# First attention: the row sums and the division of a unit go behind the next unit's weight scores

## The chip, the cores and the metric

The kernel runs on one core of a Trainium2 chip. It has a matrix engine (TensorE, PE in the profile; PEld are its weight loads), a vector engine (VectorE, DVE), an engine for activation functions (ScalarE, ACT), a general engine (GpSimd, POOL) and an engine that here issues transfers (SyncE, SP). Each engine runs its own instructions in the order in which the program gives them, and waits where an instruction needs another engine's result or a buffer that is still in use. The metric is the device time of one execution in microseconds (us).

## The reference, cut to what matters

The program is a decoder of two layers on an input of 8 batches of 256 tokens and 512 features. Each layer has a self-attention, a second mixing step and a feed-forward part, each added to the input and normalized. The change lies in the self-attention of the first layer, a differential attention with 32 score heads of 16 features and 4 value heads of 32:

```python
q = (x @ Wq.T).reshape(bsz, tgt, 2 * H, HD)
k = (x @ Wk.T).reshape(bsz, tgt, 2 * KVH, HD)
v = (x @ Wv.T).reshape(bsz, tgt, KVH, 2 * HD)
k = jnp.repeat(k, NREP, axis=2)
v = jnp.repeat(v, 2 * NREP, axis=2)
...
scores = jnp.einsum('bhqd,bhkd->bhqk', q, k) * scale
...
scores = jnp.where(causal, scores, jnp.finfo(scores.dtype).min)
probs = jax.nn.softmax(scores, axis=-1)
attn_out = jnp.einsum('bhqk,bhkd->bhqd', probs, v)
attn1 = attn_out[:, 0::2]
attn2 = attn_out[:, 1::2]
...
attn = attn1 - lambda_full * attn2
attn = attn * jax.lax.rsqrt(jnp.mean(attn * attn, axis=-1, keepdims=True) + EPS) * ln_w
attn = attn * (1.0 - LAMBDA_INIT)
...
return attn @ Wo.T
...
x = _layernorm(x + _L0_attn_ref(x, L0_attn_Wq, L0_attn_Wk, L0_attn_Wv, L0_attn_Wo, L0_attn_lambda_q1, L0_attn_lambda_k1, L0_attn_lambda_q2, L0_attn_lambda_k2, L0_attn_ln_w), axis=-1)
```

Two later self-attentions, of the second layer, use the same code path of the kernel with other inputs.

## The kernel before, in words

`causal_attention` (line 1238 on) is written once and called three times: as "a" for the first attention, "s" for the second layer's attention and "r" for its last part. The change concerns "a". There the work is cut into 64 units. A unit is one batch of 256 tokens and four score heads, which sit on the four quarters of the 128 partitions; eight units make a batch (`upb` is 8), sixteen a group of two batches.

A unit passes through three stages at three times, each in another turn of the loop over `u`:

- `maxima(u)`: the scores with queries on the partitions (ps_q, line 1300), copied out by ACT (`rows`, line 1309), masked by POOL (line 1311) and reduced to the largest value of each query by DVE (`neg`, line 1320). At the end of a batch `split` turns these maxima into three bf16 terms (lines 1327 to 1334, six small DVE steps), and `turn` brings them to the other layout with TensorE (ps_n, line 1342).
- `weights(u - 9)`: the scores again, with keys on the partitions (ps_k, line 1363), less the maxima (line 1372); ACT takes the exponential (`pT`, line 1380), POOL masks it (line 1381) and adds two of its blocks (line 1391), so that one product can sum the rest.
- `products(u - 10)`: the weights times the values (ps_pv, line 1406), then the weights times ones (line 1416), which gives the sum of each row; DVE takes the reciprocal (line 1424) and divides. In "a" this is `gather`: an even unit's result is written with line 451; an odd unit's, times minus lambda, goes to `second` (line 454), and POOL adds it (line 455). After a batch's last unit `finish` prepares the row norm: ACT squares (line 575), TensorE sums (line 527), POOL takes the roots (line 556, 8 columns each, four steps on different turns), ACT widens them (line 552), TensorE turns them and DVE multiplies (line 572); then the batch's two output blocks (ps_o) are made, added to x and normalized (`add_norm_later`).

ps_q and ps_k have the same name of buffer, "sc", of four banks, and there is one. So each waits until ACT has emptied the other. The buffer of ps_pv, one bank, is also single, except in the last batch.

The loop writes the order by hand, by Python at the time of the build. In each turn of `u` it gives: events of "start", `maxima`, some filling work, `products` (through `sums`), events of "mid", `weights`, more filling work (projections of the next batches, output blocks, transposes; a cost is kept for each and a budget `rate` of at least 2.4 a turn), `turn` after a batch's end, the rest of the filling, the reduction of the maxima, `split`, and events of "end". `at(n, place, f)` books `f` for n turns later. After 64 turns there are no more maxima, and ten more turns finish the last batch in another order: weights, products, "mid", filling.

In the last group the context is transposed too (`turn_context`): the eight even tiles go to a buffer that stays, the eight odd ones to `cT`, and each is written to memory by a transfer that SP issues (line 442).

Of the kernel before, what the change touches and what calls it, by code (L numbers as in the profile page):

```python
# [17 lines left out]
F32 = mybir.dt.float32  # L18
BF16 = mybir.dt.bfloat16
AF = mybir.ActivationFunctionType  # L20
ALU = mybir.AluOpType
# [3 lines left out]
P = 128  # L25
B, S, D = 8, 256, 512
NT = B * S // P
# [3 lines left out]
KB = D // P  # L31
# [22 lines left out]
def decoder_kernel(ctx: ExitStack, tc: tile.TileContext, a: dict, out: bass.AP):  # L54
    nc = tc.nc
# [236 lines left out]
    def diff_attention(xh, ch):  # L292
# [142 lines left out]
        def turn_context(work, pools, i):  # L435
            t = order[i]
            if t % 2:
                c = work.tile([P, KB, P], F32, tag="cT", name="cT")
            else:
                c = ch[:, :, t // 2, :]  # L440
            turned(pools, c, cx.pop(i))
            nc.sync.dma_start(out=ctx_d[:, :, t * P : (t + 1) * P], in_=c)
            if i + 2 < NT:
                load_context(work, i + 2)

        def gather(work, pools, at, yT, n, c, o, r):

            k = c // 2 % 2 * 2 + c // 4
            y = yT[:, k, :]
            if c % 2 == 0:  # L450
                nc.vector.tensor_tensor(y, o, r, ALU.mult)
                return
            d = work.tile([P, S], F32, tag="second", name="second")
            nc.vector.scalar_tensor_tensor(d, o, nlam, r, ALU.mult, ALU.mult)
            nc.gpsimd.tensor_tensor(y, y, d, ALU.add)
            if n < B - 1:
                return
            sq = squares(n)[:, k, :]

            def sums():  # L460
                ps = pools.tile([P, 2, 4], F32, tag="mm", name="ps_ss")
                for i in range(2):
                    nc.tensor.matmul(
                        ps[:, i, :], lhsT=sq[:, i * P : (i + 1) * P], rhs=quad, start=True, stop=True
                    )
                rr = small.tile([P, 2 * 4], F32, tag="rr", name="rr")
                nc.vector.tensor_scalar(
                    rr, ps.rearrange("p i t -> p (i t)"), 1.0 / 32, EPS, ALU.mult, ALU.add
                )
                wide = work.tile([P, 2 * 4, 32], F32, tag="wide2", name="wide2")  # L470
                at(0, "end", lambda: nc.gpsimd.tensor_tensor(rr, rr, neg_half[:, :8], ALU.pow))
                at(1, "mid", lambda: nc.scalar.copy(wide, rr.unsqueeze(2).broadcast_to([P, 8, 32])))
                at(1, "fill", [(TR / 2, lambda: scale(wide))])

            def scale(wide):
                pt = pools.tile([P, 2, P], F32, tag="mm", name="pt_rr")
                for i in range(2):
                    nc.tensor.transpose(
                        pt[:, i, :], wide[:, 4 * i : 4 * i + 4, :].rearrange("p t d -> p (t d)"), ident
                    )  # L480
                nc.vector.tensor_tensor(y, y, pt.rearrange("p i q -> p (i q)"), ALU.mult)

                if k == 1:
                    last.extend(out_tile(work, pools, 2 * n + i, yT, at) for i in range(2))
                    for steps in last:
                        at(0, "fill", steps[: KB - 1])
                elif k == KB - 1:
                    for steps in last:
                        at(0, "fill", steps[KB - 1 :])

            at(1, "mid", lambda: nc.scalar.activation(sq, y, AF.Square))
            at(1, "fill", [(0.4, sums)])

        last = []
# [11 lines left out]
        def finish(work, pools, t0, yT, at):  # L506
# [4 lines left out]


            apart = 1 if t0 == NT - 4 else 2
            wide = {}
            sq = squares(t0 // 2)

# [55 lines left out]
                nc.vector.tensor_tensor(y, y, pt, ALU.mult)  # L572
                at(1, "fill", out_tile(work, pools, t0 + i, yT, at))

            at(1, "start", lambda: nc.scalar.activation(sq, yT, AF.Square))
            at(1, "fill", [(0.7, sums)])
            return cost

        causal_attention("a", prepare, finish, 8, gather)
# [658 lines left out]
    def causal_attention(name, prepare, finish, upb=KB, gather=None):  # L1238
# [18 lines left out]
        with ExitStack() as st:  # L1257
# [6 lines left out]
            start = ExitStack()  # L1264
# [128 lines left out]
            def products(u):  # L1393

                g, b, c = unit(u)
                v = groups[g][2]
                p = pT.pop(u)

                late = u >= units - upb
                spare = late and u % 2  # L1400
                ps = (pools if spare else ps_pv).tile(
                    [P, 2, S], F32, tag="mm" if spare else "pv", name="ps_pv"
                )
                for j in range(2):
                    for s in range(4):
                        nc.tensor.matmul(  # L1406
                            ps[32 * s : 32 * s + 32, 0, j * P :],
                            lhsT=v(2 * b + j, 4 * c + s),
                            rhs=p[:, 1, s, :] if j else p[:, 0:3:2, s, :],
                            start=(j == 0),  # L1410
                            stop=(j == 1),
                        )
                first = p[:, 0:3:2] if late else p[:, 0:4:3]
                for j in range(2 if late else 1):
                    for s in range(4):
                        nc.tensor.matmul(  # L1416
                            ps[32 * s : 32 * s + 32, 1, j * P :],
                            lhsT=ones_v,
                            rhs=p[:, 1, s, :] if j else first[:, :, s, :],
                            start=(j == 0),  # L1420
                            stop=(j == 1 or not late),
                        )
                r = work.tile([P, S], F32, tag="rsum", name="rsum")
                nc.vector.reciprocal(r, ps[:, 1, :])  # L1424
                if c == 0:
                    yT[u // upb] = work.tile([P, KB, S], F32, tag="yT", name="yT_b")
                if gather:
                    gather(work, pools, at, yT[u // upb], u // upb, c, ps[:, 0, :], r)
                else:
                    nc.vector.tensor_tensor(yT[u // upb][:, c, :], ps[:, 0, :], r, ALU.mult)  # L1430

            upg = 2 * upb
            units = upg * NG
# [9 lines left out]
            def at(slots, place, f):  # L1443


                if place == "due mid":
                    at(slots, "mid", lambda: insort(queue, f, key=lambda piece: piece[0]))
                elif place == "fill":
                    after.append((now[0] + slots, f))
                    after.sort(key=lambda piece: piece[0])  # L1450
                else:
                    events.setdefault((now[0] + slots, place), []).append(f)

            def happen(place):
                for f in events.pop((now[0], place), []):
                    f()
# [43 lines left out]
                return most  # L1500

            def sums(u):
                nonlocal per_batch
                if lag <= u < units + lag:
                    products(u - lag)
                    if (u - lag) % upb == upb - 1:
                        n = (u - lag) // upb
                        per_batch = finish(work, pools, 2 * n, yT.pop(n), at)

            begin(0)  # L1510
            need(0)
# [5 lines left out]
            for u in range(units + lag + 2):  # L1517
                now[0] = u
                happen("start")

                rate = max(2.4, pressure(u) + per_batch / upb)
                if u < units:
                    largest = maxima(u)
                    short = max(0.0, min(0.8, rate - 1.8))
                    if rate > 2.7:
                        short += (rate - 2.7) / 2
                    left = fill(left + short)
                    sums(u)
                    happen("mid")
                    if u >= wait:  # L1530
                        weights(u - wait)
                    if u % upg == upb and u // upg + 1 < NG:
                        begin(u // upg + 1)
                    left = fill(left + rate - short - MM) - need(u + 1)

                    if u and u % upb == 0:
                        turn(u // upb - 1)
                    left = fill(left + MM)
                    largest()
                    if u % upb == upb - 1:  # L1540
                        split(u // upb)
                else:

                    if u < units + wait:
                        weights(u - wait)
                    sums(u)
                    happen("mid")
                    left = fill(left + rate) - need(u + 1)
                    if u == units:
                        turn(B - 1)  # L1550
                happen("end")
# [759 lines left out]
```

## Time and profile before

The runs took 2078.91, 2085.25 and 2088.3 us, a median of 2085.25. The profile is of an execution of its own:

| | |
|---|---|
| profiled execution | 2086.01 us |
| span from its first to its last instruction | 2084.3 us |
| PE / PEld busy | 1926.3 / 1123.2 us |
| DVE / ACT / POOL busy | 1231.7 / 617.3 / 853.7 us |
| mean granted TensorE clock | 0.982 |
| first attention, ps_q of unit 0 to the last division | 13.3 to 447 us |
| units 10 to 62, ps_q to ps_q | 54.02 to 388.71 us |

How to read it: a matmul's row has a start and a modelled end, and matmuls overlap, so the start-to-start time tells more than the duration. A number in square brackets in the order of time is the idle time of that engine before the instruction, and the name behind the arrow is the one whose result ended it. A line number is that of the kernel's listing; several operations share the line of a helper (208 is the helper that feeds projections by columns). POOL's durations are rough.

### The profile page before, as it was taken

What the parts mean: (1) busy time and instruction counts of PE and PEld (TensorE: products, weight loads), DVE (VectorE), ACT (ScalarE), POOL (GpSimd) and SP (SyncE); (2) the same over time, 40 slices, a digit from 0 to 9 for tenths busy, and PEclk for the clock granted to TensorE, in tenths of its full rate; (3) what the DMA queues carried; (4) which work ended last, traced back from release to release, by engine and by line L of the source; (5) the groups of instructions that cost most, each with busy time, mean ns of one, the idle gap of its engine ahead of it and who ended that gap; (6) DMA issues with size and microseconds to landing.
All of it is one profiled execution on the core that took longest, in us unless ns stands there. A gap on an engine that the chain in (4) does not pass through costs nothing. (4 is left out here: it accounts for less than half of the span.)

```text
span 2084.3 us, 46208 instructions
## 1 busy us (share of the span) xinstructions
PE 1926.3 (92%) x20068; PEld 1123.2 (54%) x20068; DVE 1231.7 (59%) x1876; ACT 617.3 (30%) x790; POOL 853.7 (41%) x945
## 2 busy tenths in 40 slices
PE   7979999889999999999969999998999999988885
PEld 5545555444443445656635545544878778454443
DVE  4677777658888975122225757457343442536887
ACT  4555555530000003211114334431101011245552
POOL 2677777647555833000014545344000000216763
PEclk9999999999999999999989999999999999999998
DMA  6899933316124126223122212002000000160000
GB/s 227 314 397 391 382 126 78 87 36 235 31 71 150 58 93 205 70 89 120 56 92 78 82 32 82 3 2 91 33 21 31 22 29 1 53 223 12 30 24 31
DMA packets 137467, 218.17 MB, mean 105 GB/s; under 512 B 27376, under 2 KB 52080, under 8 KB 137264
## 3 DMA queue, kind: packets, MB, share of 16 engines
q1 hardware_dynamic: 130800, 194.88, 27.0%
q0 software_dynamic: 6464, 20.32, 2.9%
q8 instruction: 160, 2.62, 0.5%
q14 instruction: 43, 0.35, 0.1%
HBM read 104.42 MB, written 123.34 MB: 109 GB/s over the span
## 5 line engine op out<-in xcount | busy, mean ns | idle before, releaser
L1424 DVE RECIPROCAL rsum<-ps_pv 128x256 f32<-128x256 f32 x128 | 224.4, 1753 | 223.3 <-PE ps_pv L1416 223.2
L178 PE MATMUL ps_y<-kv,wt 128*128 128x512 f32 x640 | 280.1, 596 | 5.2 <-POOL kv L620 2.7
L1380 ACT ACTIVATE pT<-ps_k 128x1536 f32<-128x1536 f32 x128 | 185.7, 1451 | 239.0 <-PE ps_k L1372 232.1
L1320 DVE TENSOR_REDUCE neg<-rows 128x12 f32<-128x1536 f32 x128 | 222.9, 1741 | 47.4 <-POOL rows L1311 47.4
L1309 ACT COPY rows<-ps_q 128x1536 f32<-128x1536 f32 x128 | 184.1, 1438 | 160.5 <-PE ps_q L1300 100.0
L1381 POOL TENSOR_SCALAR_AFFINE_SELECT pT<-pT 128x1024 f32<-128x1024 f32 x128 | 141.1, 1102 | 186.0 <-ACT pT L1380 185.9
L1311 POOL TENSOR_SCALAR_AFFINE_SELECT rows<-rows 128x1024 f32<-128x1024 f32 x128 | 141.0, 1101 | 159.8 <-ACT rows L1309 159.4
L178 PEld LDWEIGHTS ps_y<-kv,wt 128*128 128x128 f32 x640 | 120.8, 191 | 156.4 <-issue 137.0
L1391 POOL TENSOR_TENSOR pT<-pT 128x512 f32<-128x512 f32 x112 | 147.4, 1316 | 9.3
L1217 POOL DMA_INDIRECT first_h<-ys,slots x32 | 33.3, 1041 | 261.5 <-DMA ys<-y_m 253.9
L208 PE MATMUL ps_f<-xT,w_l1a 128*32 128x256 f32 x2048 | 124.0, 386 | 1.7 <-ACT xT L233 1.7
L1104 DVE TENSOR_TENSOR h_b<-h_b,pg 128x352 f32<-128x352 f32 x36 | 18.7, 520 | 147.2 <-ACT h_b L1103 146.4
L146 POOL TENSOR_SCALAR rstd<-bn_mv 128x1 f32<-128x1 f32 x80 | 16.6, 207 | 213.4 <-DVE bn_mv L152 209.8
L1416 PE MATMUL ps_pv<-pT,ones_v 128*32 128x256 f32 (+1 forms) x1152 | 86.2, 376 | 15.3 <-POOL pT L1391 15.1
L1125 PE MATMUL po_m<-dn,hT 128*128 (+1 forms) x216 | 98.8, 594 | 0.6 <-ACT hT L1115 0.5
L658 DVE TENSOR_REDUCE yc<-z 128x64 f32<-128x512 f32 x128 | 86.1, 673 | 5.7 <-POOL w_l1a L659 5.2
L208 PEld LDWEIGHTS ps_f<-xT,w_l1a 128*32 128x32 f32 x2048 | 62.7, 111 | 47.9 <-issue 9.6
L1300 PE MATMUL ps_q<-kz,qT 32*128 32x128 f32 x1536 | 61.5, 289 | 17.1 <-ACT pT L1380 13.8
L1300 PEld LDWEIGHTS ps_q<-kT,qT 32*128 32x128 f32 x1536 | 48.6, 186 | 51.1 <-ACT pT L1380 17.5
L1300 PE MATMUL ps_q<-kT,qT 32*128 32x128 f32 x1536 | 60.8, 287 | 14.1 <-ACT pT L1380 8.6
L1300 PEld LDWEIGHTS ps_q<-kz,qT 32*128 32x128 f32 x1536 | 49.2, 188 | 45.7 <-ACT pT L1380 32.1
L1363 PE MATMUL ps_k<-qT,kT 32*128 32x256 f32 (+1 forms) x1024 | 69.6, 358 | 4.5 <-ACT pT L1380 2.2
(386 smaller groups left out, 3620.4 us busy)
## 6 DMA issues: line engine op xcount, KB each, us to landing
xs<-zero SPq DMA_DIRECT2D x8, 4352.0 KB
ys<-zero SPq DMA_DIRECT2D x8, 4352.0 KB
filters<-in_L_xattn_k SPq DMA_DIRECT2D x4, 2560.0 KB
first_h<-xs SPq DMA_DIRECT2D x36, 256.0 KB
ys<-y_m SPq DMA_DIRECT2D x36, 256.0 KB
gu<-in_L_ffn_gate_up_proj SPq DMA_DIRECT2D x3, 2816.0 KB
wt<-filters SPq DMA_DIRECT2D x32, 256.0 KB
sorted_x<-zero SPq DMA_DIRECT2D x1, 5120.0 KB
```

Source lines behind the costliest of these rows:

```text
L178: nc.tensor.matmul(ps, lhsT=lhsT(k), rhs=rhs(k), start=(k == 0), stop=(k == n - 1))
L208: nc.tensor.matmul(ps[cs], lhsT=lhsT[:, cs], rhs=rhs, start=start, stop=stop)
L1125: nc.tensor.matmul(po, lhsT=hT[:m, i, :], rhs=dn[i][:m, bass.ds(e, 1), :], start=(i == 0), stop=(i == len(FCH) - 1),)
L1300: nc.tensor.matmul(block[:, s, j, :], lhsT=q(rows, c, b * S + i * P, P), rhs=k(rows, c, b * S + keys * P, P), start=True, stop=True,)
L1309: nc.scalar.copy(d.rearrange("p j s k -> p s j k"), block)
L1311: nc.gpsimd.affine_select(out=rows, in_=rows, compare_op=ALU.is_ge, fill=-FAR, base=0, pattern=[[0, 8], [-1, P]], channel_multiplier=1,)
L1320: return lambda: nc.vector.tensor_reduce(neg[u // upb % 2][:, :, :, c], d, AX.X, ALU.max, negate=True)
L1380: nc.scalar.activation(p[:, 0:3].rearrange("p j s q -> p s j q"), block, AF.Exp)
L1381: nc.gpsimd.affine_select(out=p[:, 0:2].rearrange("p j s q -> p (j s) q"), in_=p[:, 0:2].rearrange("p j s q -> p (j s) q"), compare_op=ALU ...
L1391: nc.gpsimd.tensor_tensor(p[:, 3], p[:, 1], p[:, 2], ALU.add)
L1416: nc.tensor.matmul(ps[32 * s : 32 * s + 32, 1, j * P :], lhsT=ones_v, rhs=p[:, 1, s, :] if j else first[:, :, s, :], start=(j == 0), stop= ...
L1424: nc.vector.reciprocal(r, ps[:, 1, :])
```

## The change

`products` is cut in two. The values products stay where they were. The ones products, the reciprocal, the new yT tile and the division (with `gather`) become a function `divided` that `products` returns; `sums` returns it together with the batch's `finish` as `rest`. In "a" the main loop calls `rest`, and then the events of "mid", after `weights`; in "s" and "r", and in the last ten turns of "a", it calls it at once, so the order there is the old one.

The row norm's start moves with it: for all batches of `finish` but the last it handles (`hurry`, batch 6), Square is booked for the end of the next turn instead of its start, and the sums product for the turn after that instead of the next. Three buffer counts change: yT has three in "a" instead of two, cT one instead of two, and the last batch's widened roots, "wide2", use the buffers of "wide".

```diff
-                c = work.tile([P, KB, P], F32, tag="cT", name="cT")
+                c = work.tile([P, KB, P], F32, tag="cT", name="cT", bufs=1)
...
-                wide = work.tile([P, 2 * 4, 32], F32, tag="wide2", name="wide2")
+                wide = work.tile([P, 2 * 4, 32], F32, tag="wide", name="wide2")
...
+            hurry = t0 == NT - 4
...
-            at(1, "start", lambda: nc.scalar.activation(sq, yT, AF.Square))
-            at(1, "fill", [(0.7, sums)])
+            at(1, "start" if hurry else "end", lambda: nc.scalar.activation(sq, yT, AF.Square))
+            at(1 if hurry else 2, "fill", [(0.7, sums)])
...
-                first = p[:, 0:3:2] if late else p[:, 0:4:3]
-                for j in range(2 if late else 1):
-                    for s in range(4):
-                        nc.tensor.matmul(
-                            ps[32 * s : 32 * s + 32, 1, j * P :],
-                            lhsT=ones_v,
-                            rhs=p[:, 1, s, :] if j else first[:, :, s, :],
-                            start=(j == 0),
-                            stop=(j == 1 or not late),
+                def divided():
+                    first = p[:, 0:3:2] if late else p[:, 0:4:3]
+                    for j in range(2 if late else 1):
+                        for s in range(4):
+                            nc.tensor.matmul(
+                                ps[32 * s : 32 * s + 32, 1, j * P :],
+                                lhsT=ones_v,
+                                rhs=p[:, 1, s, :] if j else first[:, :, s, :],
+                                start=(j == 0),
+                                stop=(j == 1 or not late),
+                            )
+                    r = work.tile([P, S], F32, tag="rsum", name="rsum")
+                    nc.vector.reciprocal(r, ps[:, 1, :])
+                    if c == 0:
+                        yT[u // upb] = work.tile(
+                            [P, KB, S], F32, tag="yT", name="yT_b", bufs=3 if name == "a" else 2
                         )
-                r = work.tile([P, S], F32, tag="rsum", name="rsum")
-                nc.vector.reciprocal(r, ps[:, 1, :])
-                if c == 0:
-                    yT[u // upb] = work.tile([P, KB, S], F32, tag="yT", name="yT_b")
-                if gather:
-                    gather(work, pools, at, yT[u // upb], u // upb, c, ps[:, 0, :], r)
-                else:
-                    nc.vector.tensor_tensor(yT[u // upb][:, c, :], ps[:, 0, :], r, ALU.mult)
+                    if gather:
+                        gather(work, pools, at, yT[u // upb], u // upb, c, ps[:, 0, :], r)
+                    else:
+                        nc.vector.tensor_tensor(yT[u // upb][:, c, :], ps[:, 0, :], r, ALU.mult)
+
+                return divided
...
-                if lag <= u < units + lag:
-                    products(u - lag)
+                if not lag <= u < units + lag:
+                    return lambda: None
+                divided = products(u - lag)
+
+                def rest():
+                    nonlocal per_batch
+                    divided()
                     if (u - lag) % upb == upb - 1:
                         n = (u - lag) // upb
                         per_batch = finish(work, pools, 2 * n, yT.pop(n), at)
+
+                return rest
...
-                    sums(u)
-                    happen("mid")
+                    rest = sums(u)
+                    if name != "a":
+                        rest()
+                        happen("mid")
                     if u >= wait:
                         weights(u - wait)
+                    if name == "a":
+                        rest()
+                        happen("mid")
...
-                    sums(u)
+                    sums(u)()
                     happen("mid")
```

More of the change, by code (lines that the diff above doesn't have):

```diff
@@ L1502, in sums @@
             def sums(u):
-                nonlocal per_batch
-                if lag <= u < units + lag:
-                    products(u - lag)
+                if not lag <= u < units + lag:
[4 more added lines that the diff above has]
+                    divided()
                     if (u - lag) % upb == upb - 1:
```

## The prediction, made before the run

> **What bounds the kernel now.** I read the share of busy time first (PE 92%, so time can only come out of TensorE's idle parts), then the 40 slices, where the first attention, up to about 447 us, holds the low digits the change can reach, then the waits by line there, then the order of time of single units. The change touches no loop outside this attention, so its window decides; this is that window, units 10 to 62, and what the rest of the kernel has beside it.
>
> ```profile
> 54.00:388.70 334.70, 300.58 (x5528) 170.27 (x5524) 247.88 (x265) 187.35 (x180) 247.10 (x230) 0.99 0.74 269
> 388.70:447.00 58.30, 50.34 (x798) 29.13 (x794) 40.70 (x56) 25.92 (x31) 33.13 (x34) 1.00 0.23 67
> ```
>
> The columns are the stretch, its length, and the busy time of PE, PE's weight loads, DVE, ACT and POOL. In 53 units of 6.31 us PE idles for 34 us; no engine is full. So a chain bounds a unit, and the order of time of unit 52 shows which (start, duration, engine, line, output and inputs, idle time before it and who ended it):
>
> ```profile
> 319.15 0.95 PE L1300 MATMUL ps_q<-kz,qT 32*128 32x128 f32 x24
> 320.17 1.44 ACT L1309 COPY rows<-ps_q 128x1536 f32<-128x1536 f32 x1 [0.96 <-PE ps_q L1300]
> ...
> 320.62 1.27 POOL L1391 TENSOR_TENSOR pT<-pT 128x512 f32<-128x512 f32 x1
> ...
> 321.94 0.64 PE L1416 MATMUL ps_pv<-pT,ones_v 128*32 128x256 f32 x8 [0.50 <-POOL pT L1391]
> 322.51 0.71 PE L1363 MATMUL ps_k<-qT,kz 32*128 32x256 f32 x8
> 322.65 1.76 DVE L1424 RECIPROCAL rsum<-ps_pv 128x256 f32<-128x256 f32 x1 [2.32 <-PE ps_pv L1416]
> ...
> 323.74 1.45 ACT L1380 ACTIVATE pT<-ps_k 128x1536 f32<-128x1536 f32 x1 [2.13 <-PE ps_k L1372]
> ...
> 325.84 0.76 PEld L1300 LDWEIGHTS ps_q<-kz,qT 32*128 32x128 f32 x24 [0.41 <-ACT qT L1567]
> ```
>
> The two score products share one buffer. The next ps_q waits for the exponential (L1380) to empty it, ps_k for the copy (L1309). The copy ends at 321.61, yet ps_k starts at 322.51: PE stands in order behind the ones products, and these wait for POOL's sum (L1391), which ends at 321.89. That is 0.90 us in which ACT waits for nothing but PE's order. The waits of the window say the same (total, times, longest):
>
> ```profile
> ACT pT L1380 <- PE ps_k L1372: 96.4, 52, 3.1
> DVE rsum L1424 <- PE ps_pv L1416: 75.6, 43, 3.7
> ...
> PEld ps_q L1300 <- ACT pT L1380: 31.3, 35, 2.1
> ...
> PEld ps_pv L1416 <- POOL pT L1391: 17.8, 28, 0.9
> ```
>
> At unit 49 nothing stood in the way: ps_q at 301.19, ps_k at 303.70, next ps_q at 306.43. So a unit has two halves with floors: A, ps_q to ps_k, 2.51 us (1.02 to the copy, 1.44 copy, 0.05), and B, ps_k to the next ps_q, 2.73 us (1.23, 1.45, 0.05).
>
> **The change, part by part.** *Ones behind ps_k.* I took A and B of units 10 to 62 from the order of time: A sums to 172.1 us (mean 3.25), B to 162.6 (3.07). PE's own work in each half I counted by start-to-start times: ps_q 0.87 us, values products 0.65, ones 0.55, ps_k 0.92, eight ps_f 0.43, eight ps_o 0.87, four transposes 0.56. Without its ones, A's work exceeds 2.51 us in only five units, and the sum of the larger of work and floor is 134.2: 37.9 us saved. B gets 0.55 more work; in 40 units work then exceeds 2.73 us, and the sum of the larger of both is 170.2: 7.7 us lost. Net 30.3 us, or 5.74 us a unit. This is also near all of PE's 34 us, so it is the upper end, and I now take off what comes late.
>
> *Reciprocal and division.* Now the reciprocal starts 0.14 us after ps_k starts; then it is 0.92 + 0.64 + 0.07 + some 0.08 = 1.71 us after. As ps_k is 0.72 us earlier (37.9/53), DVE's start is about 0.85 us later against the rest of the unit. DVE's order is unchanged, so all behind it moves too: the division (0.42 or 0.48), "mid" norms (L161, 0.56), the reduction (1.74), at a batch's end the split. The division now ends 1.71 + 1.75 + 0.45 = 3.91 us after ps_k. Its PSUM buffer is single, so the next values products wait for it; they must start by the next ps_q plus 1.86 (2.51 - 0.65) to hold up nobody, that is 3.21 + 1.86 = 5.07 us after ps_k in the mean, 4.59 in the shortest B. Slack 0.7 to 1.1 us, so nothing is lost where DVE is on time. DVE is not on time at a batch's end:
>
> ```profile
> 140.27 1.27 POOL L1391 TENSOR_TENSOR pT<-pT 128x512 f32<-128x512 f32 x1
> 140.62 0.97 DVE L1327 TENSOR_TENSOR neg<-neg 128x32 f32<-128x32 f32 x1
> ...
> 142.60 1.02 DVE L1331 CAST terms<-less 128x64 bf16<-128x64 f32 x1
> ...
> 143.54 1.74 DVE L1424 RECIPROCAL rsum<-ps_pv 128x256 f32<-128x256 f32 x1
> 144.08 0.29 PE L1342 MATMUL ps_n<-ident_b,terms 128*32 128x128 bf16 x8
> ```
>
> Here (unit 24) the reciprocal comes 1.30 us after its ones; the first units of the other batches show 0.80, 1.30, 2.82, 1.58 and 1.49. With some 0.65 us more, unit 24's division ends at 146.4, where the next values products could start at 145.5: 0.9 us lost, times 6 batches, 5 us. The turn of the maxima (ps_n) needs the same split: bounds are nothing (144.08 was not held up) and 1.3 us (0.85 and the 0.55 by which PE gets there sooner, less what is idle); I take 0.5, 3 us in six. Other units where DVE has res, statistics and norm together (0.69 + 0.69 + 0.18 + 0.56): 2 us.
>
> The row above also shows why the split is long: the minimum takes 0.97 us beside POOL's sum and ends with it, where 0.20 us is its length alone; six small steps take 2.84 us instead of 1.24. I leave the split at its present length; its ends are 1.6 us shorter and about 0.8 us longer (one more step held), 10 us less to 5 us more in six, of which only the part beyond the slack counts. [...]
>
> *POOL.* L455 (0.74 us) moves behind L1381 and L1391. That frees these two (POOL stood 25.0 + 11.3 us before L455, in front of them), and makes L455, a root (1.65) behind it and the next rows select start up to 0.6 to 2.3 us later. POOL's 4.6 us of a unit still fit 5.74; the select's reader (reduction) is last in DVE's unit. I put zero, with 2 us either way.
>
> *Square and sums.* Square (1.06 us) goes from the front of a unit, where it waited 2.2 us for L455 in five batches, to its end, behind the exponential. It runs in ACT's hole of 1.07 us before the rows copy; with one evacuation beside it (0.38) the copy is 0.4 us late: 2.4 us in six batches. The sums product, which waited 1.8 us for Square in unit 26, comes a unit later and no longer waits (that wait is inside the 37.9).
>
> *A unit later in the tail.* Batch 5's second output block (32 matmuls, 3.5 us of PE) moves one unit deeper into units 64 to 73, where PE is busy 50.3 of 58.3 us: between 0 and 3.5 us, I take 2. The tail's own order is unchanged.
>
> *Buffers.* The third yT buffer removes a wait that never showed. One cT buffer makes ACT's copy of an odd context tile wait for the former's transfer. Copies lie 3.1 us or more apart; the closest pair (407.11, 410.20) has its transfer issued at 407.72, and the DMA engines are busy until about 410.2. So 0 to 1 us once, with ACT 44% busy behind it: nothing. The root's copies sharing one tag meet only in the tail: nothing.
>
> Sum: -30.3 + 5 + 3 + 2 + 2.4 + 2 = -15.9 us. The profiled execution took 2086.0 us (span 2084.3), 0.8 above the median shown. 2086.0 - 15.9 = **2070 us**. The stage's end moves the rest with it: the long convolution starts on the last norms (465 us), and the DMA engines, busy with zeros up to some 300 us, have only 23% in the tail.
>
> **The rivals.** *All of it:* nothing is late, 2086 - 30 = 2056. For it: 75.6 us of DVE's idle time before the reciprocal. Against: batch ends.
>
> *Given back at batch ends:* the lag of unit 40 (2.82 us) at all six, so each costs 2.82 + 0.65 - 1.1 for the values products and as much again for the turn, 4.7 us x 6 = 28 us instead of 8: 2090; with half of that, 2076. For it: DVE's load at a batch's last unit, 1.75 + 0.45 + 1.74 + 2.9 = 6.8 us, is over the new 5.74.
>
> *Slower, DVE takes the chain everywhere:* each division's lateness beyond its slack of 1.1 us goes into the next unit, 53 times. It decides from a mean lag of 1.1 + 26/53 = 1.6 us in every unit; at 1.8 us the stage loses 37 and keeps 26: 2097. For it: DVE at 4.7 of 5.74 us, and a reciprocal that may no longer start early. Against: today 40-odd units show 0.07 us of lag, and the ring reciprocal, division, values, ps_k, ones needs only 4.6 us.
>
> *Held by the write-back:* cT's copies wait 2.5 us each for their transfer in a tail that ACT then sets, 7 x 2.5 us: 2087. Against: ACT's 44%.
>
> **How the numbers follow.** Forecast (2060 to 2075) 0.50; all of it 0.07; given back 0.23, between 2076 and 2090; slower 0.14; write-back 0.06. Faster by over 0.5% (about what a measurement can tell from no change; below 2075 us): 0.50 + 0.07 + a little of the third, 0.59. Slower (over 2096): 0.14. Same: 0.27. The range of 8 in 10 takes in both batch-end cases: 2056 to 2094; the forecast's own is 2060 to 2076.
>
> **What would show it.** Right: ps_k 0.05 us behind the copy in most units, ps_q about 5.7 us apart, the reciprocal some 1.7 us behind ps_k's start, PE's wait for L1391 gone. Wrong: values products waiting for L451 or L454, ps_n for the split, the copy for Square, DVE without idle time ahead of the reciprocal, or a tail beyond 58 us.

## The result, and the profile after

The changed kernel takes 2074.34 us in the median (2071.3 to 2077.54), 0.9954 of the time before with a 95% interval of 0.9941 to 0.9967: by this ratio 9.6 us less (the two medians differ by 10.9). The gain is small, but the interval leaves no change out. The forecast was 2070, a ratio of 0.9923 against the profiled execution before. The profiled execution after took 2074.25 us (span 2072.5).

The table of stretches for the same stage, from the profile after: units 10 to 62, then unit 63 to the last division. The columns are the stretch, its length, the busy time of PE, PE's weight loads, DVE, ACT and POOL with the number of instructions, the granted clock, and the DMA engines.

```profile
55.20:383.30 328.10, 300.24 (x5512) 175.63 (x5508) 253.61 (x261) 188.18 (x179) 244.77 (x228) 0.98 0.75 275
383.30:442.70 59.40, 52.11 (x810) 29.66 (x810) 43.19 (x59) 26.10 (x31) 35.96 (x36) 1.00 0.24 66
```

PE has the same 300 us of work, in 328.1 us instead of 334.7. A unit takes 6.19 us in the mean, not the 5.7 that was to be seen. PE still idles for 28 us, so the stage is still no engine's.

What was to happen does happen. In the order of time of unit 20, up to the start of unit 21, where PE has no filling work (start, duration, engine, line; in brackets the idle time before it and who ended it):

```profile
112.53 0.95 PE L1301 MATMUL ps_q<-kz,qT 32*128 32x128 f32 x24 [0.67 <-ACT pT L1381]
113.55 1.44 ACT L1310 COPY rows<-ps_q 128x1536 f32<-128x1536 f32 x1 [1.07 <-PE ps_q L1301]
...
115.04 0.71 PE L1364 MATMUL ps_k<-qT,kz 32*128 32x256 f32 x8 [0.20 <-ACT rows L1310]
...
116.07 0.64 PE L1418 MATMUL ps_pv<-pT,ones_v 128*32 128x256 f32 x8
...
116.78 1.76 DVE L1426 RECIPROCAL rsum<-ps_pv 128x256 f32<-128x256 f32 x1 [1.19 <-PE ps_pv L1418]
117.77 0.95 PE L1301 MATMUL ps_q<-kz,qT 32*128 32x128 f32 x24 [1.06 <-ACT pT L1381]
118.57 0.42 DVE L451 TENSOR_TENSOR yT_b<-ps_pv,rsum 128x256 f32<-128x256 f32 x1
```

ps_k starts 0.05 us after the copy's end (114.99), the ones products come behind it, the reciprocal starts 1.74 us after ps_k, and the unit takes 5.24 us, exactly the two floors of 2.51 and 2.73. The waits of the window say it for all units (total, times, longest):

```profile
DVE rsum L1426 <- PE ps_pv L1418: 70.5, 39, 4.3
ACT pT L1381 <- PE ps_k L1373: 65.1, 49, 3.1
...
PEld ps_k L1364 <- ACT rows L1310: 20.4, 48, 1.0
PEld ps_q L1301 <- ACT pT L1381: 15.6, 15, 1.5
...
PE pt_ss L541 <- DVE means L535: 5.3, 2, 3.0
...
PEld pt_ss L541 <- DVE means L535: 3.4, 1, 3.4
```

ACT's wait for ps_k fell from 96.4 to 65.1 us, the wait of the ones products for POOL's sum (17.8 us before) is gone, and ps_k now waits for the copy itself in nearly every unit. But ps_q waits for the exponential in 15 loads of weights instead of 35: in the other units the half from ps_k to the next ps_q is now ended by something else. The halves, read from the starts in the order of time as the prediction did, tell how much:

| units 10 to 62, us | before | forecast | after |
|---|---|---|---|
| A, ps_q to ps_k | 172.1 | 134.2 | 139.2 |
| B, ps_k to the next ps_q | 162.6 | 170.2 | 189.0 |
| both | 334.7 | 304.4, and 12.4 for lateness: 316.8 | 328.2 |
| from ps_q of unit 63 to the last division | 58.3 | 60.3 | 59.4 |

A came as forecast, all but 5.0 us. B missed by 18.8 us. Three kinds of place can be read off, some in B and some in A. The first is unit 35, with 6.3 us from ps_k (208.40) to the next ps_q (214.69), again in the order of time:

```profile
208.40 0.71 PE L1364 MATMUL ps_k<-qT,kz 32*128 32x256 f32 x8
...
209.43 0.64 PE L1418 MATMUL ps_pv<-pT,ones_v 128*32 128x256 f32 x8
...
210.13 1.76 DVE L1426 RECIPROCAL rsum<-ps_pv 128x256 f32<-128x256 f32 x1 [0.87 <-PE ps_pv L1418]
...
210.74 0.61 PE L528 MATMUL ps_ss<-w_l,quads 128*32 128x256 f32 x8
...
211.93 0.48 DVE L454 SCALAR_TENSOR_TENSOR second<-ps_pv,nlam,rsum 128x256 f32<-128x256 f32 x1
...
212.33 0.68 DVE L268 TENSOR_TENSOR res<-ps_o,x 128x512 f32<-128x512 f32 x1
213.04 0.69 DVE L151 BATCH_NORM_STATS2 bn_st<-res 128x6 f32<-128x512 f32 x1
...
213.87 0.39 DVE L535 TENSOR_SCALAR means<-ps_ss 128x256 f32<-128x256 f32 x1
...
214.32 0.44 PE L541 MATMUL pt_ss<-ident,means 128*128 128x128 f32 x2 [2.96 <-DVE means L535]
214.69 0.95 PE L1301 MATMUL ps_q<-kz,qT 32*128 32x128 f32 x24
```

The row norm's sums product (L528) was filled in behind ps_k. Its means (L535) stand on DVE behind reciprocal, division, res and statistics, 3.74 us in all from 210.13, and the norm's transposes (pt_ss, L541), booked for the same turn's end, stand on PE ahead of the next ps_q. So PE waits 2.96 us with the next unit behind it. Unit 59 shows the same (2.33 us). Their B is 3.23 and 2.73 us more than the larger of work and floor; together 6.0 us. In units 19, 28, 44 and 52 the sums product lies in A, ahead of ps_k, and PE does not wait for the means. In units 10 to 62 of the kernel before the same wait of PE was there, but small: 1.1 us in three places.

The second is unit 25:

```profile
143.56 1.72 DVE L1426 RECIPROCAL rsum<-ps_pv 128x256 f32<-128x256 f32 x1
...
145.66 0.68 DVE L573 TENSOR_TENSOR yT_b<-yT_b,pt_rr 128x512 f32<-128x512 f32 x1
...
146.48 1.07 PE L208 MATMUL ps_o<-w_l,yT_b 128*32 128x512 f32 x8 [1.76 <-DVE yT_b L573]
```

The output block needs the scaled yT (L573), which DVE makes behind the reciprocal of the turn that follows the split. PE stands 1.76 us, in A. With unit 41 this is 3.5 us.

The third is the clock. Units 21, 22 and 36 lie where the granted clock is 0.50 (the stretches are shown at the end), and are 4.7 us longer than the larger of work and floor. Before has such a place too, in unit 60 (0.51 from 370.7 to 374.2 us).

### The profile page after: what moved, and what is told of

The parts are those of the page before. It is cut to its first block, busy times and chain, and to the rows that moved or that the text cites. A ratio compares the mean times of both kernels' runs of the same rounds, so it can differ in the third digit from the quotient of the medians.

```text
span 2072.5 us, 46201 instructions
## 1 busy us (share of the span) xinstructions
PE 1926.8 (93%) x20068; PEld 1127.2 (54%) x20068; DVE 1239.6 (60%) x1876; ACT 618.9 (30%) x790; POOL 853.6 (41%) x945
## 5 line engine op out<-in xcount | busy, mean ns | idle before, releaser
L1381 ACT ACTIVATE pT<-ps_k 128x1536 f32<-128x1536 f32 x128 | 185.8, 1452 | 211.8 <-PE ps_k L1373 202.1
L1312 POOL TENSOR_SCALAR_AFFINE_SELECT rows<-rows 128x1024 f32<-128x1024 f32 x128 | 141.1, 1102 | 160.0 <-ACT rows L1310 159.6
L1364 PE MATMUL ps_k<-qT,kz 32*128 32x256 f32 (+1 forms) x1024 | 69.4, 358 | 9.0 <-ACT rows L1310 8.8
```

Of the source, the lines that this page charges most:

```text
L1312: nc.gpsimd.affine_select(out=rows, in_=rows, compare_op=ALU.is_ge, fill=-FAR, base=0, pattern=[[0, 8], [-1, P]], channel_multiplier=1,)
L1364: nc.tensor.matmul(block[:, s, at, :], lhsT=k(rows, c, b * S + j * P, P), rhs=q(rows, c, b * S + j * P, P * (2 - j)), start=True, stop=False,)
L1381: nc.scalar.activation(p[:, 0:3].rearrange("p j s q -> p s j q"), block, AF.Exp)
```

## The experiments

Compared in the table is the stage from ps_q of unit 10 to the last division, from one profiled execution of each, worked out from the starts; the ratio is against the kernel before on the same chip. The runs were made on more than one chip: after_again, old_order and square_early on one, the next four rows on another, the last two on a third.

| kernel | A | B | stage | ratio [95%] |
|---|---|---|---|---|
| before | 172.1 | 162.6 | 392.9 | 1 |
| before_again | 171.5 | 165.4 | 396.7 | one run |
| after | 139.2 | 189.0 | 387.6 | 0.9954 [0.9941, 0.9967] |
| after_again | 139.6 | 187.9 | 386.9 | 0.9954 [0.9940, 0.9968] |
| old_order | 167.5 | 169.8 | 396.2 | 0.9999 [0.9990, 1.0008] |
| square_early | 163.2 | 196.7 | 419.7 | 1.0091 [1.0076, 1.0107] |
| norms_later | 142.9 | 181.6 | 384.5 | 0.9938 [0.9916, 0.9959] |
| out_later | 138.8 | 194.8 | 395.0 | 1.0013 [0.9999, 1.0027] |
| both_later | 140.1 | 183.0 | 381.9 | 0.9924 [0.9899, 0.9949] |
| balanced | 142.1 | 172.1 | 371.9 | 0.9874 [0.9851, 0.9897] |
| norms_balanced | 150.1 | 166.8 | 376.7 | 0.9914 [0.9895, 0.9933] |
| balanced_old | 179.1 | 159.1 | 396.6 | 1.0011 [0.9998, 1.0023] |

**The two kernels once more.** No edit; both are profiled again to learn what a single profile can tell.

> The changed kernel once more, nothing edited. In the first pair of profiles the span from ps_q of unit 10 to the last division of the first attention went from 392.9 to 387.6 us (-5.4), its end came 4.2 us earlier, and the whole execution 11.8 us. So 7.5 us of the profiles' difference fell behind the stage, in code that the change leaves alone: 3.7 us in one step near 820 us, 3 us in the second attention. Theory 1 (the change is worth what the stage shows, the rest differs between single executions): the stage again 387 to 389 us; the part behind the stage moves by several us against the first profile; ratio of the times between 0.994 and 0.998. Theory 2 (the whole 11.8 us is the change's, for instance by where the code lies): the same steps at the same places, 0.994 to 0.995.

> The kernel before once more, for a second profile of it. Theory 1 (differences behind the stage are those of single executions): stage 392 to 394 us as before; the step near 820 us (ACT's copy idle for 5.79 us) is gone or elsewhere, and the time behind the stage differs from the first profile by 3 us or more. Theory 2: it is at the same place with the same length.

after_again gives a median of 2076.49 us and the same ratio; its halves agree with the first profile to about 1 us. The second profile of before does not agree with its first so well:

```profile
54.95:391.79 336.84, 303.27 (x5529) 172.21 (x5525) 248.04 (x264) 187.35 (x180) 247.14 (x230) 0.98 0.73 267
```

Its stage is 3.8 us longer, with a granted clock of 0.98 instead of 0.99, and what lies outside the stage is 1686.6 us (2083.34 less 396.7) instead of 1693.1, as in the profiles after (1686.7 and 1685.1). So the first profile of before was short in the stage and long outside it, and the stage alone gains 5.3 us by the first pair and 9.8 by the second; the ratio's 9.6 agrees with the latter. Differences of some 4 us between single profiles mean nothing here.

**What of the change does it: the order, or Square and the buffers?** old_order keeps the late Square and the buffers, and calls the rest at once as before:

```diff
                     rest = sums(u)
-                    if name != "a":
-                        rest()
-                        happen("mid")
+                    rest()
+                    happen("mid")
                     if u >= wait:
                         weights(u - wait)
-                    if name == "a":
-                        rest()
-                        happen("mid")
```

> The changed kernel with the ones products, reciprocal, division and mid events ahead of the weight scores again; the later Square and sums and the buffers stay. Theory 1 (the reorder carries the gain, A halves): A of units 10 to 62 back near 170 us of the 139, stage near that of before, 390 to 394 us, time 2081 to 2088. Theory 2 (the gain is Square's and the sums product's later place, 2.4 + 2.5 us of waits that went away): stage 386 to 389, time 2073 to 2078.

0.9999: nothing. The buffers and the late Square neither give nor cost by themselves, and the gain is the order's. In square_early the order is the new one, and Square and the sums product stand where they stood:

```diff
-            hurry = t0 == NT - 4
+            hurry = True
```

> The changed kernel with Square at the start of the next turn and the sums product in its filling, as before the change, for every batch; the new order stays. Theory 1 (Square must follow the addition L455, which now comes behind the select and the sum): Square waits on ACT ahead of the rows copy, the copy of that unit comes 2 to 3 us late, in six batches 12 to 18 us, less the wait of the norm's transposes (7 us) that goes: stage 392 to 400 us, time 2079 to 2087. Theory 2 (the place of Square does not matter, and the norm's transposes are the larger loss): stage 381 to 385 us, time 2067 to 2072.

2106.25 us, 29.8 more than after_again on the same chip, and more than expected. The order of time of unit 26 of square_early:

```profile
154.52 0.72 POOL L455 TENSOR_TENSOR yT_b<-yT_b,second 128x256 f32<-128x256 f32 x1
155.27 1.06 ACT L576 ACTIVATE w_l<-yT_b 128x1024 f32<-128x1024 f32 x1 [1.77 <-POOL yT_b L455]
...
156.24 1.42 ACT L1310 COPY rows<-ps_q 128x1536 f32<-128x1536 f32 x1
156.38 0.16 PEld L528 LDWEIGHTS ps_ss<-w_l,quads 128*32 128x32 f32 x8 [3.19 <-ACT w_l L576]
```

Square waits for the last addition of the batch (L455), which now comes late, and the rows copy stands behind Square on ACT: it starts 3.81 us after its ps_q (152.43) instead of 1.02, and PE waits 3 us in front of the sums. So the later Square is no side issue: without it the change would be slower than before.

**Do the norm's transposes and the output blocks eat the gain?** norms_later books the transposes for the middle of the next turn (all batches but the last of `finish`):

```diff
-                at(0, "end", norms)
+                at(0, "end", norms) if hurry else at(1, "mid", norms)
```

> The changed kernel with the norm's transposes (pt_ss) booked for the middle of the next turn instead of the end of the same one. Theory 1 (in the changed kernel PE stands at pt_ss for 2.96 and 2.33 us in units 35 and 59, because the means wait on DVE behind the later reciprocal; 7 us with the smaller ones): the waits go, units 35 and 59 fall from 8.8 and 9.1 to about 6 us, the half-clock window near 214 us that follows the first of them goes too (1 us); stage 379 to 382 us instead of 387, time 2066 to 2070. Theory 2 (the time is then lost at the next late step, since DVE is what is late): stage 385 to 388, time 2073 to 2077.

out_later leaves the transposes and books the output blocks a turn later, so that ps_o does not stand in front of L573's end:

```diff
-                at(1, "fill", out_tile(work, pools, t0 + i, yT, at))
+                at(1 if hurry else 2, "fill", out_tile(work, pools, t0 + i, yT, at))
```

> The changed kernel with the output blocks two turns behind the multiplication by the roots instead of one, batch 6 left as it is. Theory 1 (in units 25 and 41 ps_o waits for DVE's multiplication L573, which lies behind a reciprocal that the split has made late; 1.85 and 1.65 us): these two units fall to about 6 us, stage 383 to 385 us, time 2070 to 2074. Theory 2 (the division's lateness, which holds the values products there as well, takes over): stage 386 to 388, no change of time.

What PE and its weight loads waited for ahead of the norm's transposes, from the view of that tile, in after, in norms_later and in out_later:

```profile
its engine sat idle before it (us, times) until:
  DVE means L535: 10.1, 4
```

```profile
its engine sat idle before it (us, times) until:
...
  DVE means L535: 0.3, 1
```

```profile
its engine sat idle before it (us, times) until:
  DVE means L535: 19.8, 7
```

The columns are microseconds and times; a stall shows on PE and on its weight loads, so it is counted up to twice. These three views cover the whole run, the last ten turns of the attention too; PE's own share of the wait in units 10 to 62 is 5.3 us in after, nothing in norms_later and 8.3 us in out_later. In norms_later B falls by 7.4 us: the two units had cost 6.0, and the low clock behind the first of them, 0.9 us of B, is gone too. But A rises by 3.7, and the stage gives 2.5 to 3 us, less than expected: four units of 7.8 to 9.5 us (26, 28, 42, 44) are new or longer, and the output blocks' wait for L573 is still there, 4.9 us in three. By time it can't be told from the change (0.9938 against 0.9954, with intervals that overlap). out_later cures what it was made for: units 25 and 41 fall to 6.0 us. As a whole it fails: the output blocks, a turn later, come ahead of the sums product in the filling, so that this falls behind ps_k in one more batch (unit 51), and the transposes' wait grows by 3 us. Three units (35, 51, 59) take 8.8 to 9.1 us. It loses all of the gain; the grown wait explains a part of that. Then both edits together:

> Both edits, norm's transposes and output blocks later. Theory 1: the two gains add, 5 to 7 and 2 to 4 us: stage 376 to 380 us, time 2063 to 2068, unless the work that moves into the last ten turns makes them longer than 59.4 us by 2 us. Theory 2: no better than the better of the two.

0.9924, a stage of 381.9, short of what was expected; by time it can't be told from norms_later (the intervals overlap). PE's waits for the means and for L573 are both gone from units 10 to 62. But this profile has a place of another kind: unit 57 takes 12.25 us, since PE waits 3.64 us there for a transfer of the context (`cx`) in front of a transpose, and the granted clock is 0.50 from 340.7 to 347.5 us. A unit of some 6 us in its place would give a stage of about 376 (an estimate).

**Is it also where the filling is put?** With the ones gone from A, A's work is 2.0 to 2.4 us in most units, below its floor of 2.51, while B's is 3.2 to 3.7 in most, above 2.73. The budget of the first filling (`short`) is 0.6 us at the least rate of 2.4. balanced is both_later and a first filling of 0.9 at least, so that about 0.3 us a unit goes from B to A:

```diff
+                    if name == "a":
+                        short = max(short, 0.9)
                     left = fill(left + short)
```

> Both edits, and in the first attention a filling of at least 0.9 instead of 0.6 between ps_q and the values products, so that work moves from B (where PE has 0.55 us of ones more than before and sets the end in 40 of 53 units) to A (where PE has 1.96 us of work for a floor of 2.51 in half of the units). Theory 1 (after the change B is bound by PE, A by ACT's copy): B falls by up to 0.43 us in some 25 to 35 units, 8 to 12 us, A stays within 3 us: stage 366 to 372 us, time 2054 to 2060. Theory 2 (more work in A delays the values products and with them ps_k as much as it helps B): no better than with both edits alone.

Units 10 to 62 of balanced in the table of stretches, and its waits there:

```profile
58.00:372.10 314.10, 296.44 (x5508) 172.36 (x5504) 252.08 (x261) 186.52 (x178) 241.24 (x226) 0.99 0.78 285
```

```profile
ACT pT L1381 <- PE ps_k L1373: 67.7, 51, 2.6
...
PEld ps_q L1301 <- ACT pT L1381: 24.8, 29, 1.5
```

53 units in 314.1 us, 5.93 each; ps_q waits for the exponential in 29 loads, against 15 in after, so the exponential ends B in more units; in the others the filling still does. Against both_later, with unit 57 left out of both, A pays 5.3 us for B's 9.0. The ratio is 0.9874 [0.9851, 0.9897], below both others: against after (0.9954, on another chip) by another 0.8%, against both_later by 0.5%, and no interval touches the other. The single profiles show less of the step from both_later, under 4 us in these units without unit 57, which is no more than two profiles of one kernel differ by.

Which of balanced's parts are needed? norms_balanced leaves the output blocks where they were:

```diff
-                at(0, "end", norms)
+                at(0, "end", norms) if hurry else at(1, "mid", norms)
...
+                    if name == "a":
+                        short = max(short, 0.9)
```

> The changed kernel with the norm's transposes a turn later and a filling of at least 0.9 ahead of the values products; the output blocks stay one turn behind. Theory 1 (moving the output blocks was worth nothing: 1.0013 alone, 0.9924 against 0.9938 with the norm's transposes): ratio as that of the version with all three edits, 0.985 to 0.990, stage 370 to 375 us. Theory 2 (the output blocks' wait for L573 costs where A is filled more): 3 us or more worse, 0.989 to 0.992.

0.9914, and A is 8 us longer than in balanced. Its waits show why: PE waits for L573 ahead of ps_o for 7.2 us in four places, and in balanced nowhere. So the output blocks' place is worth some 5 us of the stage once the rest is done, although alone it lost. The ratios, from two chips, don't show it (their intervals overlap at the edge). balanced_old puts the same filling into the kernel before:

```diff
+                    if name == "a":
+                        short = max(short, 0.9)
                     left = fill(left + short)
```

> The kernel before with the filling of at least 0.9 ahead of the values products and nothing else. Theory 1 (the room for work in A is opened by the change alone: before it, the ones products and their wait for L1391 stand there): A grows by what is moved, up to 0.43 us in 25 units, B falls by no more, ratio 0.998 to 1.008. Theory 2 (the split of the filling was poor before, too): stage 380 to 387 us, ratio 0.992 to 0.997.

1.0011 [0.9998, 1.0023]: nothing. A grows by 7.0 us and B shrinks by 3.5. In the old order the ones stand in A, and A pays for what it is given; the room is the change's own. The old order with all three edits was not run.

**How much slack has the division?** Both kernels with the first attention's reciprocal computed twice, into the same place:

```diff
-                nc.vector.reciprocal(r, ps[:, 1, :])
+                for _ in range(2 if name == "a" else 1):
+                    nc.vector.reciprocal(r, ps[:, 1, :])
```

> The changed kernel with the reciprocal of the first attention done twice, 1.75 us more on DVE in each unit. It measures the slack that the prediction gave the division (0.7 to 1.1 us). Theory 1 (slack is as worked out): the values products wait for the division in every unit, 0.65 to 1.05 us each, units 10 to 62 take 34 to 58 us more than 328, 362 to 386. Theory 2 (DVE has no slack any more, it is the bound): 1.75 us each, 420 us. Theory 3 (the lateness is covered): under 340 us.

> The kernel before with the reciprocal done twice. By the prediction its reciprocal starts 1.57 us earlier against ps_k, so its slack is about 2.2 to 2.7 us and 1.75 us of more work fit: DVE gets 6.45 us of work for units of 6.31. Theory 1: units 10 to 62 take 341 to 355 us, 7 to 20 more. Theory 2 (no slack before either): 1.75 us each, 425 us.

The new order takes 399.6 us for units 10 to 62, 71 more, and beyond the 362 to 386 expected. The values products now wait for the division in most units, 0.15 us after its end. The slack itself was worked out well: the second reciprocal adds 1.79 us (3.55 against 1.76), and in units 11 and 13 to 17, where nothing else is late, A grows by 0.8 to 1.1, so that 0.7 to 1.0 was slack. What the expectation lacked stands elsewhere. PE's wait for the norm's means goes from 5.3 to 8.9 us, that of the output blocks for L573 from 3.4 to 8.8, that of PE's weight loads for the terms of the maxima from 3.1 to 8.4: the places that were late in after already. The granted clock is lower too, 0.94 in these units instead of 0.98. In double_after's waits, from 54 to 412 us:

```profile
PE ps_pv L1407 <- DVE yT_b L451: 22.8, 21, 2.3
PE ps_pv L1407 <- DVE second L454: 17.9, 16, 2.3
```

The old order was expected to bear it better and did not: 412.6 us, 78 more. It does bear it in every second unit: in 13, 15 and 17 A stays at 2.96 us, while in 12, 14 and 16, where it was 3.0 to 3.4 us, it is 4.7 to 5.6. The latter are the turns right behind one that wrote `second`. Its waits, from 54 to 412 us, show another way by which a late division reaches PE:

```profile
POOL yT_b L455 <- DVE second L454: 57.7, 18, 4.9
...
PEld ps_pv L1406 <- POOL pT L1381: 42.1, 23, 3.6
```

POOL's addition L455 stands there ahead of the next select L1381, so when `second` is late, POOL waits, the select is late, and the values products wait for the select. In the new order L455 comes behind select and sum, and this way is closed.

## Why the prediction was right or wrong

*Ones behind ps_k, half A: right.* 37.9 us forecast, 32.9 measured; the 6 us or so of A above the larger of work and floor are units 25 and 41 (3.5, ps_o behind L573), 22 and 36 (2.05, low clock), and a rest of small ones.

*Half B: the step that failed.* Forecast 7.7 us more, measured 26.4. The prediction took B as the larger of work and floor, which leaves out every wait in PE's order other than the exponential's, and it set this sum against B as measured before, which has such waits in it. Counted with the same costs, B of the kernel before comes to some 152 us, where 162.6 were measured; so about 10 us were taken off by the way of counting, without a reason. Of the 18.8 us, 2.6 are the sum itself (over the filling as it lies after it is about 172.8, not 170.2); 6.0 the norm's transposes (units 35 and 59); 2.6 the low clock; 1.05 the turn of the maxima in unit 56; 0.7 a projection's first matmuls in unit 44, 0.49 us apart for a reason that the profile doesn't show. The remaining 5.9 lie in some 34 units, 0.1 to 0.4 us in each, and in many of them PE's work was counted too small: in unit 13, with the ones and 32 ps_f, the prediction's costs give 3.19 us and B takes 3.33. The starts there are 1.03 us from ps_k to the ones, 0.46 to the first ps_f and 1.84 from that to ps_q, where 0.92, 0.55 and 1.72 were counted. The kernel before has the same (unit 13: 2.64 counted, 2.90 measured).

*Values products at six batch ends, 5 us: nothing.* Where DVE is late they start 0.15 us after the division, and ps_k is not held up. In units 25 and 41 PE comes to them late anyway, behind the output block, so these two can't show it.

*The turn of the maxima, 3 us: about 1* (unit 56).

*Other lateness of DVE, 2 us: mis-sized.* This term should have held the norm's transposes and the output blocks, 6.0 and 3.5 us. The terms for lateness of DVE together came to 10 us, and what was found is 10.5: the sum was near by luck, the places were not. Both that cost have one pattern: a matmul that PE meets in its order soon after the DVE step that feeds it, when that step now stands behind a reciprocal 1.76 us long that starts later. The prediction asked who waits for the division, and not who waits for what stands behind it on DVE.

*The split beside POOL, between 10 us less and 5 us more, left out of the sum: no worse.* The six splits' steps take 2.0 to 2.1 us each instead of 2.0 to 3.0. In each one step takes 0.96 to 1.07 us, where the other five take 0.19 to 0.23, and it ends 0.04 to 0.06 us behind POOL's select of the rows (L1312); before there was one such step in three of the six splits and two in the other three, behind the same select or POOL's sum. So the new order brought no more of them; what makes such a step long, these runs do not show.

*Square before the rows copy, 2.4 us: nothing.* The copy starts 1.02 us after ps_q's start in those units. *POOL, zero: right*, and the move of L455 even closes a way by which DVE held up PE. *cT, zero: right* (its copies wait for PE's transposes alone). *The tail, 2 us: 1.1*, which is less than the 1.5 us by which two profiles of the kernel before differ there (58.3 and 59.8).

*Low clock: no term.* 4.7 us of the profile after lie there, in units 21, 22 and 36. Both kernels have such places, so it is not shown to be the change's; only the place in unit 36 lies right behind a wait that grew with the change.

In sum: 16 us were forecast, 9.6 measured (6.9 to 12.3). The time of 2074 us lies within 2060 to 2076, where the forecast had it, but only just, and luck has a part in that. The forecast put all of the 16 us into the stage; the stage gained 5.3 us in the first pair of profiles, and the other 6.5 us between these two executions lay outside it. In the second pair the stage gained 9.8. The rival "all of it" fell with B. "Given back at batch ends" named the right kind of place and a result close to the measured one (2076), by another way than it gave: values products and maxima cost 1 us, the norm and the output blocks 9.5. "Slower, DVE takes the chain everywhere" fell: the reciprocal's lag is 0.07 us in most units, and doubling it shows what it would have taken. What supports the mechanism best is balanced beside balanced_old: with these waits gone and the filling moved the new order gains 1.3%, and the old order with the same filling, though without the other two edits, nothing. Units 10 to 62 of balanced take 314.2 us, near the forecast's 316.8, but with another order of the filling than the forecast had in view.

## What to carry to other kernels

When work is moved to a later place on one engine, list what stands behind it on that engine and, for each, the instruction of the bounding engine that reads it and its place in the order; a sum of floors sees none of these waits. Work taken out of one half of a loop leaves room there that nothing fills by itself: move the filling too, or part of the gain stays unspent (0.9924 became 0.9874 here). An edit that loses alone can gain once the wait it feeds is gone (the output blocks, by PE's waits in norms_balanced and balanced), so it is worth trying again in company. A sum of costs and floors should first be held against the kernel before, whose halves are measured: here it was 10 us short there.

## What the runs showed of the hardware that was not expected

Up to 452 us of the profile after PE's granted clock fell to 0.50 in stretches of 3.4 us (from 48.6 and from 215.8 us), or of two or three times that (6.8 us from 444.5, 10.3 us from 120.2). Some of that profile's stretches, with the columns of the first fence:

```profile
116.80:120.20 3.40, 1.63 (x40) 1.18 (x40) 3.37 (x3) 2.33 (x2) 3.32 (x4) 1.00 1.05 408
120.20:130.50 10.30, 9.68 (x116) 5.63 (x108) 4.96 (x5) 3.83 (x5) 9.01 (x8) 0.50 1.04 401
144.10:147.50 3.40, 1.64 (x36) 0.92 (x32) 3.37 (x4) 1.85 (x2) 2.88 (x4) 1.00 0.89 348
147.50:150.90 3.40, 3.40 (x63) 1.75 (x56) 1.53 (x2) 1.45 (x1) 0.03 (x1) 1.00 1.05 407
212.40:215.80 3.40, 1.48 (x30) 1.12 (x34) 3.33 (x6) 0.10 (x1) 2.59 (x4) 1.00 0.96 369
215.80:219.20 3.40, 3.40 (x44) 2.05 (x40) 0.22 (x2) 1.34 (x1) 2.70 (x2) 0.50 1.05 408
```

In the 3.4 us ahead of the two low stretches PE was busy for 1.63 and 1.48 us. The stretch from 212.4 us on is the stall of unit 35, and the low clock right behind it lies in unit 36; in norms_later, where that wait is gone, the clock from 215.8 to 219.2 us is whole (1.00). So in this pair of profiles the low clock of unit 36 came and went with the wait of unit 35. PE's busy time in the 3.4 us ahead does not tell the cases apart: with 1.64 us of work, from 144.1 to 147.5, the clock stayed whole, and with 1.63 it fell. What sets the clock these profiles do not show.

The other is double_before's: in the order where POOL stood between DVE and PE a slower DVE step cost 78 us, in the order where PE waits for DVE itself 71. These are one profile each, at granted clocks of 0.92 and 0.94, and so small a difference shows no order between them; that the first isn't the cheaper one was not expected.
